# Layer 0 of a graph network: bias rows of two projections added by GpSimd, values projected third, source tile by integer, one-hots from bf16 numbers

## The chip, the core and the metric

The kernel runs on one core of one Trainium2 chip. The core has a matrix engine (TensorE, PE in the profile), VectorE (DVE), ScalarE (ACT), GpSimd (POOL) and a queue for transfers (SyncE, SP). Matrix products land in PSUM, everything else on chip lies in SBUF. The metric is the device time of one execution in microseconds (us). The kernel before takes 1515.7 us, the median of three runs (1515.66 to 1519.37).

## The reference

1250 nodes with 512 features pass through two layers. Each layer adds a graph convolution, a linear attention and a mixture of experts to the features. The change touches the front of layer 0 and the routing in layer 1. Cut to that:

```python
xn = _layernorm(x)                       # x: [1250, 512]
# layer 0, graph convolution: 20000 edges, mean over the edges into a node
h_self = xn @ W_self.T
neigh_sum = segment_sum(xn[src], dst)
h = h_self + (neigh_sum / max(deg, 1)) @ W_neigh.T + bias        # then a layer norm
# layer 0, attention on a normalised row hn
q = sigmoid(hn @ Wq + bq); k = sigmoid(hn @ Wk + bk); v = hn @ Wv + bv
# layer 1 uses the same edges with weights
agg = segment_sum(h1[src] * norm, dst)
# layer 1, experts: the two best of 8 experts for each token, mixed by softmax gates
topk_vals, topk_idx = top_k(logits, 2); gates = softmax(topk_vals)
```

## The kernel before, in words

The nodes are cut into T = 10 tiles of P = 125 rows. The first phase, which the change is about, does two things at once for each tile `t`:

- **Five projections**, listed in `kinds`: y (the neighbour term, applied before the sum over edges), z (the own term), q, k and v. Each is four f32 products of 128 rows by 512 columns into a PSUM tile `pm` (two buffers), and each such product runs as two passes. For z, q, k and v a fifth product `row_vector` adds the bias row: a one-hot column picks one row of `row_parts`, in which every bias row is held as three bf16 parts that `split_rows` makes. ScalarE evicts `pm` into a buffer `o` of a ring with five buffers (a sigmoid for q and k), GpSimd sums q and k into `totals`, and `move_rows` stores `o` to memory in two pieces on SP. y and z work on `xt`, the transposed normalised rows, the others on `ht`, the transposed rows `hr` of a second normalisation; `normal_rows` and `turn` make these for tile t + 1 while tile t is projected.
- **The adjacency matrix** `at`, from the edges: 320 chunks of 125 edges, in 40 groups of 8. For a group VectorE compares the numbers 0 to 127 (`iota_s`) with each edge's row in its source tile (`lo_s`), which gives the one-hot `hs`, and the numbers 0 to 79 with its column (`col_w`), which gives `hm`. ScalarE multiplies `hm` by the top part of the edge weight, GpSimd by two lower parts (line 400). Per chunk PE multiplies `hs` with the parts of `hm` (lines 424 and 427) into one of four PSUM buffers `pa`, and VectorE adds the result into `at` (line 429).

PE's order in this phase is written out by hand: the loop deals out chunks between the projections' products. On the other engines a planner of the framework orders the instructions, by its own costs.

In front of the loop stands the preparation. The edges are loaded, turned into columns (`as_columns`), and VectorE computes each edge's source tile `tile_s` (lines 350 to 352: one comparison per tile boundary, nine in all), the row in it `lo_s`, and the column `col_w`. The five weights and the first rows of x are queued on SP; the weights lie in one large buffer `big`, in the order neighbour, self, q, k, v. Later y and q are loaded back into the same buffer, `reload`, as soon as the weights that lie there are done with.

At the end of the loop the totals are summed over the rows (line 481) and a loop for edges that fit no window follows; it runs no round here, but all engines meet at it, and SP's transfers issued before it have to land. Then come the products with `at` (line 633).

In layer 1 the routing makes lists: for every block of 128 places which token stands where. `listed` makes one-hots of places (`hotp`) and blocks (`blk`), multiplies the blocks by the numbers to be listed (`hotb`), and PE sums them up. The first list gives `row_i`, by which GpSimd gathers rows; the second (`value`: tile, row, a one, and the gate in three bf16 parts, made through `part_b`) gives target rows and gates.

Of the kernel before, what the change touches and what calls it, by code (L numbers as in the profile page):

```python
# [8 lines left out]
F32 = mybir.dt.float32  # L9
# [11 lines left out]
P = 125  # L21
T = N // P
D = 512
# [47 lines left out]
def gps_two_layer_kernel(ctx: ExitStack, tc: tile.TileContext, x, src, dst, ew, rows, cols,  # L71
# [138 lines left out]
    with ExitStack() as phase:  # L210
# [4 lines left out]
        iota_s = gp.tile([CH, 128], F32, name="iota_s")  # L215
# [5 lines left out]
        lo_s = gp.tile([CH, NC], F32, name="lo_s")  # L221
        col_w = gp.tile([CH, NC], F32, name="col_w")
# [6 lines left out]
        full = ring.tile([96, D], F32, name="full", tag="o", bufs=5)  # L229
# [57 lines left out]
        with tc.tile_pool(name="eprep", bufs=1) as ep, \  # L287
# [68 lines left out]
            inside = ep.tile([CH, NC], F32, name="inside", tag="f", bufs=3)  # L356
# [6 lines left out]
            split_rows(row_parts, full, ring, tag="o", bufs=5)  # L363
# [70 lines left out]
        def fill(n):  # L434
            for _ in range(n):
                if fills:
                    m, t = fills.pop()
                    nc.scalar.activation(at[:, m, t, :], zero.to_broadcast([128, NA]), AF.Copy)

        kinds = ((y_d, 0, wn_sb, None, AF.Copy), (z_d, 0, ws_sb, R_GNN, AF.Copy),  # L440
                 (q_d, 1, wq_sb, R_BQ0, AF.Sigmoid), (k_d, 1, wk_sb, R_BK0, AF.Sigmoid),
                 (v_d, 1, wv_sb, R_BV0, AF.Copy))
        steps, step, chunk = T * len(kinds) * DC, 0, 0
        fill(8)
        with tc.manual_schedule(engines={mybir.EngineType.PE}):
            for t in range(T):
                for n, (d, which, w_sb, row, func) in enumerate(kinds):
# [6 lines left out]
                    for c in range(DC):  # L454
                        nc.tensor.matmul(pm, lhs[:, c, :], w_sb[:, c, :], start=(c == 0),  # L455
                                         stop=(row is None and c == DC - 1))
                        if row is not None and c == DC - 1:
                            row_vector(pm, row, False)
                        if c == DC - 1:
                            o = ring.tile([P, D], F32, name="o", bufs=5)  # L460
                            nc.scalar.activation(o, pm, func)
                            move_rows(of_tile(d, t), o)
# [662 lines left out]
    with tc.tile_pool(name="moe", bufs=1) as ep:  # L1125
# [4 lines left out]
        with tc.tile_pool(name="rt", bufs=1) as rt, tc.tile_pool(name="rx", bufs=3) as rx, \  # L1130
                tc.tile_pool(name="rps", bufs=2, space=PSUM) as ps:
            iota_p = rt.tile([P, 128], F32, name="iota_p")
            nc.gpsimd.iota(iota_p, pattern=[[1, 128]], base=0, channel_multiplier=0,
                           allow_small_or_imprecise_dtypes=True)
            edges_b = rt.tile([P, NB], F32, name="edges_b")
# [3 lines left out]
            tok = rt.tile([P, T, 2], F32, name="tok")  # L1139
# [302 lines left out]
```

## Time and profile before

| what | value |
| --- | --- |
| median of the runs | 1515.7 us (1515.66, 1515.70, 1519.37) |
| profiled execution, its own time | 1518.06 us |
| its span, first to last instruction | 1516.4 us |
| mean granted clock of PE | 0.963 |
| DVE `hs`, line 387, 125x1024, median | 1.224 us |
| DVE `hm`, line 394, 125x640, median | 0.817 us |
| DVE addition into `at`, line 429 | 0.319 us, 320 of them |
| POOL low part, line 400, 125x640, median | 1.252 us, 80 of them |
| POOL addition to `totals`, line 468, 125x512, median | 1.404 us, 18 of them |
| ACT eviction, line 461, 125x512, median | 0.597 us |

The page of the profile starts with the busy time of each engine:

```profile
PE 1396.3 (92%) x6082; PEld 873.9 (58%) x6082; DVE 585.7 (39%) x1425; ACT 404.9 (27%) x937; POOL 199.1 (13%) x176
```

and goes on with 40 equal slices of the span. Each digit is the busy share in tenths, so the first eight columns are about the first 300 us:

```profile
PE   5999999999999799999965898898999999999997
DVE  8887777789775683343565000000000000000000
POOL 3355455300000000000005000000000000000000
```

PEld are PE's weight loads, which run beside its products. A row of a group reads: line, engine, operation, output<-inputs, shapes and count, then busy us in all and mean ns of one, then the idle time of that engine just before them and what ended it. A row in order of time begins with the start in us from the span's start and the duration. Durations overlap where an engine starts an instruction before the last one has left it, so what an instruction costs is read from the starts.

### The profile page before, as it was taken

The page shows a single profiled execution, that of the slowest core. Times are in us where ns is not written, and L with a number is a line of the kernel's source. Part 1 is how long each engine was busy: PE and PEld are TensorE (multiplying, and loading weights), DVE is VectorE, ACT ScalarE, POOL GpSimd, SP SyncE. Part 2 cuts the span into 40 slices and gives each one's busy share as a digit, 9 for nine tenths or more (in the row PEclk, how much of TensorE's full clock was granted, in tenths as well). Part 3 has the DMA queues.
Part 4 walks back from the last instruction along what each step waited for, and adds up shares of the span by engine and source line. Part 5 has one row for each costly group of instructions (what it writes and reads, how often), then busy time and mean ns, then how long its engine had stood idle before and what let it go on. Part 6 is the DMA issues. An engine that isn't in the chain of part 4 may idle for free. (4 is left out here: it accounts for less than half of the span.)

```text
span 1516.4 us, 18431 instructions
## 1 busy us (share of the span) xinstructions
PE 1396.3 (92%) x6082; PEld 873.9 (58%) x6082; DVE 585.7 (39%) x1425; ACT 404.9 (27%) x937; POOL 199.1 (13%) x176
## 2 busy tenths in 40 slices
PE   5999999999999799999965898898999999999997
PEld 2445445424554346554534696884767567975673
DVE  8887777789775683343565000000000000000000
ACT  8655455201223422112224121220212012120110
POOL 3355455300000000000005000000000000000000
PEclk9999999999999899999976999999999999999999
DMA  7311111622510130001149456601542106001011
GB/s 223 104 55 56 54 55 49 194 65 89 174 47 11 35 127 1 1 0 41 48 169 340 165 187 235 225 9 38 200 157 82 14 6 233 12 7 14 1 14 15
DMA packets 72765, 134.74 MB, mean 89 GB/s; under 512 B 8328, under 2 KB 9720, under 8 KB 72622
## 3 DMA queue, kind: packets, MB, share of 16 engines
q1 hardware_dynamic: 67694, 122.47, 23.8%
q0 software_dynamic: 4928, 10.43, 3.6%
q8 instruction: 81, 1.33, 0.4%
q14 instruction: 62, 0.51, 0.1%
HBM read 107.27 MB, written 26.38 MB: 88 GB/s over the span
## 5 line engine op out<-in xcount | busy, mean ns | idle before, releaser
L1329 PE MATMUL po<-w,big 128*128 128x512 f32 x576 | 250.1, 592 | 0.0
L1306 PE MATMUL pm<-hts,big 128*128 x960 | 184.8, 355 | 19.7 <-issue 17.3
L1318 DVE TENSOR_SCALAR o<-po,to_gate 128x512 f32<-128x512 f32 (+1 forms) x24 | 17.7, 749 | 454.1 <-PE po L1331 452.8
L1306 PEld LDWEIGHTS pm<-hts,big 128*128 128x128 f32 x960 | 167.0, 196 | 39.5 <-issue 24.1
L1329 PEld LDWEIGHTS po<-w,big 128*128 128x128 f32 x576 | 109.1, 190 | 132.1 <-issue 131.5
L1309 ACT ACTIVATE big<-pm,cols_sb 128x256 f32<-128x256 f32 (+2 forms) x224 | 96.1, 432 | 282.6 <-PE pm L1306 282.4
L1306 PE MATMUL pm<-hts,w 128*128 x832 | 144.8, 336 | 12.6 <-PEq L1389 5.6
L1306 PEld LDWEIGHTS pm<-hts,w 128*128 128x128 f32 x832 | 133.0, 197 | 23.8 <-issue 14.4
L455 PE MATMUL pm<-big,ht 128*125 128x512 f32 x240 | 130.3, 631 | 0.0
L1319 POOL DMA_INDIRECT out_dram<-o,row x24 | 36.9, 1539 | 652.1 <-DVE o L1318 284.9
L429 DVE TENSOR_TENSOR at<-at,pa 128x160 f32 x320 | 102.0, 319 | 41.4 <-PE pa L427 17.6
L400 POOL TENSOR_TENSOR hm<-hm,w_low 125x640 bf16<-125x640 bf16 x80 | 100.3, 1274 | 114.0 <-DVE hm L394 63.4
L123 PE MATMUL pm<-w,at 128*125 128x512 f32 x240 | 114.2, 598 | 0.0
L397 ACT ACTIVATE hm<-hm,w_top 125x80 bf16<-125x80 bf16 x320 | 86.4, 350 | 68.0 <-DVE hm L394 55.1
L633 PE MATMUL pn<-big,at 125*125 125x512 f32 x200 | 92.5, 621 | 3.0 <-DMA big<-q_d 3.0
L455 PE MATMUL pm<-big,xt 128*125 128x512 f32 x160 | 86.8, 633 | 1.2 <-ACT xt L278 1.2
L1309 ACT ACT_TABLE_LOAD x11 | 14.1, 1283 | 255.2 <-PE pm L1306 255.2
L427 PEld LDWEIGHTS <-hs 125*128 125x128 bf16 x640 | 50.8, 97 | 48.8 <-issue 44.0
L424 PE MATMUL pa<-hm,hs 125*128 125x160 bf16 x320 | 64.6, 233 | 12.9 <-DVE at L429 10.9
L424 PEld LDWEIGHTS <-hs 125*128 125x128 bf16 x320 | 31.1, 97 | 67.7 <-issue 38.4
L633 PEld LDWEIGHTS pn<-big,at 125*125 125x125 f32 x200 | 38.5, 196 | 54.7 <-issue 54.6
L427 PE MATMUL pa<-hm,hs 125*128 125x80 bf16 x640 | 64.4, 198 | 0.0
(391 smaller groups left out, 1621.2 us busy)
## 6 DMA issues: line engine op xcount, KB each, us to landing
w<-in_w_dram SPq DMA_DIRECT2D x52, 1024.0 KB
big<-in_w_dram SPq DMA_DIRECT2D x12, 1024.0 KB
x_t<-in_x_dram SPq DMA_DIRECT2D x10, 224.0 KB
xn_d<-xr SPq DMA_DIRECT2D x10, 224.0 KB
y_d<-o SPq DMA_DIRECT2D x10, 224.0 KB
z_d<-o SPq DMA_DIRECT2D x10, 224.0 KB
q_d<-o SPq DMA_DIRECT2D x10, 224.0 KB
k_d<-o SPq DMA_DIRECT2D x10, 224.0 KB
```

The source lines that it names most:

```text
L123: nc.tensor.matmul(ps, lhs[:, c, :], w[:, c, :], start=(c == 0), stop=(row is None and c == DC - 1))
L397: nc.scalar.activation(hm[:, j, 1, :], hm[:, j, 0, :], AF.Copy, scale=w_top[:, g * J + j:g * J + j + 1])
L400: nc.gpsimd.tensor_tensor(hm[:, :, 2 + i, :], hm[:, :, 0, :], w_low[:, i, c8, None].to_broadcast([CH, J, TW]), ALU.mult)
L424: nc.tensor.matmul(pa.rearrange("p k c -> p (k c)"), hs[:, j, :], hm[:, j, 0:2, :].rearrange("p k c -> p (k c)"), start=True, stop=False)
L427: nc.tensor.matmul(pa[:, 1, :], hs[:, j, :], hm[:, j, 2 + i, :], start=False, stop=(i == 1))
L429: add = nc.vector.tensor_tensor(to, to, pa.rearrange("p k (t w) -> p k t w", t=T), ALU.add)
L455: nc.tensor.matmul(pm, lhs[:, c, :], w_sb[:, c, :], start=(c == 0), stop=(row is None and c == DC - 1))
L633: nc.tensor.matmul(pn, at[:P, 0, s, t * P:(t + 1) * P], y[:, s, :], start=(s == 0), stop=(s == T - 1))
L1306: nc.tensor.matmul(pm[:, :width], w1s[e, f // DC][:, c, (f % DC) * 128:(f % DC + 1) * 128], hts[:, c, bass.ds(start, width)], start=(c == ...
L1309: nc.scalar.activation(hid[f][:, :width], pm[:, :width], AF.Gelu, bias=cols_sb[:, C_B11 + e * FC + f:C_B11 + e * FC + f + 1])
L1319: nc.gpsimd.indirect_dma_start(out, bass.IndirectOffsetOnAxis(ap=row[:n], axis=0), o[:n], None, bounds_check=N - 1, oob_is_err=False, comp ...
L1329: nc.tensor.matmul(pm, hid[f][:, s * 128:(s + 1) * 128], w2s[e, f // DC][:, f % DC, :], start=(f == 0), stop=False)
```

## The change

Four things, in one edit:

1. The bias rows of z and v no longer go through PE for each tile. `spread_row` makes each of them once into a full 125x512 tile (one row product and one eviction on ScalarE), and GpSimd adds it to the evicted `o`. For tile 0, z's `o` is held until the rows are spread, after v. The ring of `o` has four buffers instead of five.
2. v is projected third, ahead of q and k, and its weights are queued third.
3. The source tile is computed by one multiplication with conversion to an integer, a conversion back, a comparison and a subtraction, in place of nine comparisons.
4. Numbers that one-hots are made from are held in bf16: `iota_s`, `lo_s`, `col_w`, and in the routing `iota_p`, `edges_a`, `edges_b`, `tok`, `nblk`, `inb`, `blk` and `value`; the gate's parts go straight into `value`.

```diff
-        iota_s = gp.tile([CH, 128], F32, name="iota_s")
+        iota_s = gp.tile([CH, 128], BF16, name="iota_s")
...
-        lo_s = gp.tile([CH, NC], F32, name="lo_s")
-        col_w = gp.tile([CH, NC], F32, name="col_w")
+        lo_s = gp.tile([CH, NC], BF16, name="lo_s")
+        col_w = gp.tile([CH, NC], BF16, name="col_w")
...
-            for i, (o, w) in enumerate(((wn_sb, gw_neigh), (ws_sb, gw_self), (wq_sb, wq0),
-                                        (wk_sb, wk0), (wv_sb, wv0))):
+            for i, (o, w) in enumerate(((wn_sb, gw_neigh), (ws_sb, gw_self), (wv_sb, wv0),
+                                        (wq_sb, wq0), (wk_sb, wk0))):
...
-            nc.vector.tensor_scalar(tile_s, src_c, float(P), None, op0=ALU.is_ge)
-            for t in range(2, T):
-                nc.vector.scalar_tensor_tensor(tile_s, src_c, float(t * P), tile_s,
-                                               op0=ALU.is_ge, op1=ALU.add)
+
+            tile_i = ep.tile([CH, NC], I32, name="tile_i", tag="f", bufs=3)
+            nc.vector.tensor_scalar(tile_i, src_c, 0.5, 1.0 / P, op0=ALU.add, op1=ALU.mult)
+            nc.vector.tensor_copy(tile_s, tile_i)
+            up = ep.tile([CH, NC], F32, name="up", tag="f", bufs=3)
+            nc.vector.scalar_tensor_tensor(up, tile_s, float(P), src_c, op0=ALU.mult, op1=ALU.is_gt)
+            nc.vector.tensor_sub(tile_s, tile_s, up)
...
         kinds = ((y_d, 0, wn_sb, None, AF.Copy), (z_d, 0, ws_sb, R_GNN, AF.Copy),
-                 (q_d, 1, wq_sb, R_BQ0, AF.Sigmoid), (k_d, 1, wk_sb, R_BK0, AF.Sigmoid),
-                 (v_d, 1, wv_sb, R_BV0, AF.Copy))
+                 (v_d, 1, wv_sb, R_BV0, AF.Copy),
+                 (q_d, 1, wq_sb, R_BQ0, AF.Sigmoid), (k_d, 1, wk_sb, R_BK0, AF.Sigmoid))
+        spread = {}
+
+        def spread_row(row):
+            pm = ps.tile([P, D], F32, name="pm")
+            row_vector(pm, row, True, stop=True)
+            spread[row] = hmp.tile([P, D], F32, name=f"spread{row}", bufs=1)
+            nc.scalar.activation(spread[row], pm, AF.Copy)
...
                     for c in range(DC):
+                        in_psum = func is AF.Sigmoid
                         nc.tensor.matmul(pm, lhs[:, c, :], w_sb[:, c, :], start=(c == 0),
-                                         stop=(row is None and c == DC - 1))
-                        if row is not None and c == DC - 1:
+                                         stop=(not in_psum and c == DC - 1))
+                        if in_psum and c == DC - 1:
                             row_vector(pm, row, False)
                         if c == DC - 1:
-                            o = ring.tile([P, D], F32, name="o", bufs=5)
+                            o = ring.tile([P, D], F32, name="o", bufs=4)
                             nc.scalar.activation(o, pm, func)
-                            move_rows(of_tile(d, t), o)
+                            if row is not None and not in_psum:
+                                if t == 0 and n == 2:
+                                    spread_row(R_GNN)
+                                    spread_row(R_BV0)
+                                    nc.gpsimd.tensor_add(held, held, spread[R_GNN])
+                                    move_rows(of_tile(z_d, 0), held)
+                                if t == 0 and n == 1:
+                                    held = o
+                                else:
+                                    nc.gpsimd.tensor_add(o, o, spread[row])
+                            if t > 0 or n != 1:
+                                move_rows(of_tile(d, t), o)
...
-                blk = rt.tile([P, T, 2, nb], F32, name="blk", tag="blk")
+                blk = rt.tile([P, T, 2, nb], BF16, name="blk", tag="blk")
...
-            value = rt.tile([P, T, 2, 6], F32, name="value")
+            value = rt.tile([P, T, 2, 6], BF16, name="value")
...
             for i in range(3):
-                nc.vector.tensor_copy(part_b, left)
-                nc.vector.tensor_copy(value[:, :, :, 3 + i], part_b)
+                nc.vector.tensor_copy(value[:, :, :, 3 + i], left)
```

More of the change, by code (lines that the diff above doesn't have):

```diff
@@ L228, in gps_two_layer_kernel @@
         x_t = {}
-        full = ring.tile([96, D], F32, name="full", tag="o", bufs=5)
+        full = ring.tile([96, D], F32, name="full", tag="o", bufs=4)
         nc.gpsimd.memset(full, 0.0)
@@ L349, in gps_two_layer_kernel @@
             nc.gpsimd.tensor_tensor(w_low[:, 1, :], less, w_low[:, 0, :], ALU.subtract)
-            nc.vector.tensor_scalar(tile_s, src_c, float(P), None, op0=ALU.is_ge)
-            for t in range(2, T):
-                nc.vector.scalar_tensor_tensor(tile_s, src_c, float(t * P), tile_s,
-                                               op0=ALU.is_ge, op1=ALU.add)
+            tile_i = ep.tile([CH, NC], I32, name="tile_i", tag="f", bufs=3)
[4 more added lines that the diff above has]
+            nc.vector.tensor_sub(tile_s, tile_s, up)
             nc.vector.scalar_tensor_tensor(lo_s, tile_s, float(-P), src_c, op0=ALU.mult, op1=ALU.add)
             nc.vector.scalar_tensor_tensor(src_c, tile_s, float(W), where, op0=ALU.mult, op1=ALU.add)
-            inside = ep.tile([CH, NC], F32, name="inside", tag="f", bufs=3)
+            inside = ep.tile([CH, NC], F32, name="inside")
             nc.vector.tensor_scalar(inside, where, float(W), None, op0=ALU.is_lt)
@@ L362, in gps_two_layer_kernel @@
             nc.vector.memset(row_parts, 0.0)
-            split_rows(row_parts, full, ring, tag="o", bufs=5)
+            split_rows(row_parts, full, ring, tag="o", bufs=4)
             for i in range(3):
@@ L1131, in gps_two_layer_kernel @@
                 tc.tile_pool(name="rps", bufs=2, space=PSUM) as ps:
-            iota_p = rt.tile([P, 128], F32, name="iota_p")
+            iota_p = rt.tile([P, 128], BF16, name="iota_p")
             nc.gpsimd.iota(iota_p, pattern=[[1, 128]], base=0, channel_multiplier=0,
                            allow_small_or_imprecise_dtypes=True)
-            edges_b = rt.tile([P, NB], F32, name="edges_b")
+            edges_b = rt.tile([P, NB], BF16, name="edges_b")
             nc.gpsimd.iota(edges_b, pattern=[[1, NB]], base=0, channel_multiplier=0,
                            allow_small_or_imprecise_dtypes=True)
-            tok = rt.tile([P, T, 2], F32, name="tok")
+            tok = rt.tile([P, T, 2], BF16, name="tok")
             nc.gpsimd.iota(tok[:, :, 0], pattern=[[0, T]], base=0, channel_multiplier=1,
@@ L1143, in gps_two_layer_kernel @@
                            allow_small_or_imprecise_dtypes=True)
-            edges_a = rt.tile([P, NA_B], F32, name="edges_a")
+            edges_a = rt.tile([P, NA_B], BF16, name="edges_a")
             nc.gpsimd.iota(edges_a, pattern=[[1, NA_B]], base=0, channel_multiplier=0,
@@ L1183, in listed @@
                 nc.vector.tensor_single_scalar(slot_i, slot_i, 127, op=ALU.bitwise_and)
-                nblk = rt.tile([P, T, 2], F32, name="nblk", tag="nblk")
+                nblk = rt.tile([P, T, 2], BF16, name="nblk", tag="nblk")
                 nc.vector.tensor_copy(nblk, nblk_i)
-                inb = rt.tile([P, T, 2], F32, name="inb", tag="inb")
+                inb = rt.tile([P, T, 2], BF16, name="inb", tag="inb")
                 nc.vector.tensor_copy(inb, slot_i)
-                blk = rt.tile([P, T, 2, nb], F32, name="blk", tag="blk")
+                blk = rt.tile([P, T, 2, nb], BF16, name="blk", tag="blk")
                 nc.vector.tensor_tensor(blk, nblk[:, :, :, None].to_broadcast([P, T, 2, nb]),
@@ L1270, in gps_two_layer_kernel @@
             nc.vector.memset(value[:, :, :, 2], 1.0)
-            part_b = rt.tile([P, T, 2], BF16, name="part_b")
             left = rt.tile([P, T, 2], F32, name="left")
```

## The prediction

> **What bounds the kernel now.** I read the page first: the span is 1516.4 us and TensorE (PE) is busy for 92% of it, so a saved microsecond counts only where PE would otherwise work or wait. Of the change, all but the one-hots of the router lies in layer 0 before its end at about 295 us. The groups of instructions, narrowed to the engine PE and to 28 to 289 us (out<-in, count, then busy us and mean ns, then idle time in front and who ended it), show that stage:
>
> ```profile
> L455 PE MATMUL pm<-big,ht 128*125 128x512 f32 x239 | 129.9, 631 | 0.0
> L424 PE MATMUL pa<-hm,hs 125*128 125x160 bf16 x319 | 64.4, 233 | 12.9 <-DVE at L429 10.9 <-ACT o L461 1.1 <-ACT hm L397 0.5
> L101 PE MATMUL pm<-row_parts,row_pick 96*125 96x512 bf16 x39 | 15.1, 386 | 6.9 <-DVE row_parts L115 6.9
> ```
>
> See the last field. PE waits 12.9 us in front of the edge products, nearly all for VectorE (DVE) to add an earlier product into `at`, and 6.9 us once for the bias rows. The busy times per stretch, from 36 to 290 us, say how full the others are:
>
> ```profile
> 36.00:290.00 254.00, 240.65 (x1443) 126.08 (x1444) 196.16 (x441) 132.76 (x413) 122.15 (x97) 1.00 0.25 75
> ```
>
> After the stretch's length come PE 240.65, weight loads, DVE 196.16, ScalarE (ACT) 132.76, GpSimd (POOL) 122.15 of 254 us. PE sets the end, DVE is near behind, POOL is half idle.
>
> **Part 1, bias rows leave PE.** Of the 40 row products L101 in the loop, those of the own term z and of v go (20), and two come back to spread the rows once. What one costs PE is not its 0.38 us, which overlaps its neighbours, but the distance to the next start. From the order in time of PE (start, duration):
>
> ```profile
> 274.63 0.38 PE L101 MATMUL pm<-row_parts,row_pick 96*125 96x512 bf16 x1
> 274.85 0.23 PE L424 MATMUL pa<-hm,hs 125*128 125x160 bf16 x1
> ```
>
> That is 0.22 us. For tiles 1 to 9, 18 products go: 18 x 0.22 = **-4.0 us**, on the path, since PE bounds there. Tile 0's are in the ramp (part 3).
>
> In their place POOL gets 20 additions of 125x512. The nearest row is POOL's `totals` addition of the same shape, median 1.40 us (1.26 to 2.25): 28 us more on an engine with 132 us free. Two costs can come out. First, delay: POOL works in order, and an addition in front of a group's two low-part products (L400, 2.46 us) makes the group late. Setting each group's L400 end against PE's first use, I find between 0.28 and 3.5 us of slack from group 2 on, mostly 0.6 to 2.7. Today 3 of 18 additions have an L400 queued straight behind them with no gap, and PE never waits for it. In the list of POOL's instructions after the change each addition stands in front of a group that PE first uses 4.9 us or more after the addition's own projection ends; eviction 0.6, addition 1.4 and L400 2.46 make 4.5. So the order is tight in two places and wrong in none: +0.5 us, between 0 and 3.
>
> Second, contention. The order in time shows what POOL does to DVE:
>
> ```profile
> 116.13 0.82 DVE L394 TENSOR_TENSOR hm<-iota_s,col_w 125x640 bf16<-125x640 f32 x1
> 124.03 1.66 DVE L394 TENSOR_TENSOR hm<-iota_s,col_w 125x640 bf16<-125x640 f32 x1
> 123.19 1.82 POOL L468 TENSOR_TENSOR totals<-totals,o 125x512 f32<-125x512 f32 x1 [2.32 <-ACT o L461]
> ```
>
> The same DVE instruction takes 0.84 us more when an addition runs beside it, and the addition 0.4 more. The Trainium skill speaks against this part here: "GPSIMD Engine Reference", section "Specifications", says that POOL's memory interfaces are shared with VectorE and contended when VectorE reads two operands from SBUF. It gives no price; the rows do. In 36 to 290 us the one-hots L387 and L394 lie 38 x (0.059 + 0.088) = 5.6 us above their medians, and xr and hr (0.87 and 0.90 us, against 0.54 alone) 5.9 us: 11.5 us of DVE for 122 us of POOL. For 28 us more that is 2.6 us of DVE. DVE has slack and four buffers `pa`, so I take half for PE: **+1.3 us**. Bounds: 0, and by the rule with every addition hitting a one-hot 20 x 0.84 = 17 us.
>
> The ring `o` falls from 5 to 4 buffers. An `o` is made each 5.1 us and is held for eviction, addition and store, under 10 us; four are 20 us: nothing.
>
> **Part 2, one-hots from bf16 numbers.** The rows are one element a cycle: `hs` (L387, 1024 elements) 1.22 us, `hm` (L394, 640) 0.82 us, so 384 elements in 0.40 us. The change makes all operands 2-byte. The skill has two rules: "VectorE: DVE Perf Modes", "The perf-mode tier table", gives a bf16 tensor_tensor twice the rate; "Vector Engine (DVE) Microarchitecture Reference", section 5.1, says that a two-source instruction with 2-byte operands whose one input is a single element read again and again ran at the single rate. `lo_s` and `col_w` are just that: one number per chunk, repeated along the innermost axis. By the first rule DVE would lose 512/960 + 320/960 = 0.87 us per group, 35 us in all, and most of the 10.9 us of PE waits would go. By the second nothing changes. No row here has this form on DVE, and the second names the very case: **0**, bounds -9 and 0.
>
> **Part 3, the ramp.** The order in time, PE then DVE, at the start:
>
> ```profile
> 28.05 0.59 PE L101 MATMUL pm<-row_parts,row_pick 96*125 96x512 bf16 x1 [6.89 <-DVE row_parts L115]
> 36.41 0.65 PE L132 MATMUL pt<-ident,hr 125*128 125x125 f32 x4 [2.31 <-DVE hr L270]
> 30.04 1.21 DVE L253 TENSOR_TENSOR r<-mv,r 125x2 f32<-125x2 f32 x1
> 35.41 1.41 DVE L270 TENSOR_SCALAR hr<-x_t,mv,r 125x512 f32<-125x512 f32 x2
> ```
>
> PE waits 6.89 us for `row_parts` and 2.31 us for tile 1's `hr`. With v third and without its row, PE goes on at 21.2 with 8 passes of 0.43 us, so 3.4 us of projection move into the first wait. Its weights are there: the third load was issued at 15.36, and SP, whose next store waits for that load, goes on at 20.79. The tile index loses nine DVE instructions (0.31 + 8 x 0.56 = 4.8 us) and gains four (two of 0.31, two of 0.47: 1.6): -3.2. With the first `hs` (1.2 us) now behind `row_parts`, that is ready at about 24 and not 28. But the next wait, for `hr`, is set by DVE. Its new order puts after `row_parts` one set of statistics, two `hs` and two `hm` (4.9 us), then the chain from L253 to `hr`, in before 30.04 to 36.1 = 6.1 us with POOL beside it. 24.3 + 4.9 + 0.4 + 6.1 = 35.7 against 36.1. One projection, k or now q, then remains on either side. **-0.5 us**, bounds -3 (POOL out of the way) and +1.5. The spread evictions (2 x 0.6 us on ACT) lie in this wait; SP's queue meets z's store later, as in before (33.6). In the smaller ring z's eviction waits for `full`, free at 24: hidden too, 0.6 us if not.
>
> **Part 4, the joint.** k comes last instead of v. The chain behind it, ACT 0.6, POOL's total 1.27, PE 1.1, DVE 0.65, ends 4.1 us after the last projection; all engines are released later still, when SP's last loads have landed:
>
> ```profile
> 290.49 0.74 SPq L107 DMA_DIRECT2D v_d<-o  x2
> 294.78 2.07 PE L633 MATMUL pn<-big,at 125*125 125x512 f32 x2 [3.02 <-DMA big<-q_d]
> 294.00:295.00 1.00, 0.22 (x1) 0.56 0.00 0
> 295.00:300.00 5.00, 5.00 (x6) 0.50 0.74 214
> ```
>
> SP has two pieces of q instead of one to issue before that point, 0.4 us apart: **+0.4 us**, bounds 0 and 1.5. The last two rows (0.56 and 0.50 are the granted clock) show a second price: after this 3.0 us gap PE runs at half speed for about 6 us, 3 us lost. "TensorE: Matmul & The Clock Gate", Part 1, asks for a whole idle window of 3.4 us; the trace throttled with less, so the trace decides. Now k's total falls into the middle of the gap, and the clock may stay up: 0 or -3, taken as 0.
>
> **Part 5, the router.** The list chain on DVE ends with `row_i` at 793.14 and the gathers start at 793.59. Two of the removed copies (0.17 us, 0.09 apart where they interleave) stand before it: **-0.3 us**; between -2 (lists at double rate) and 0.
>
> **Sum.** -4.0 + 0.5 + 1.3 + 0 - 0.5 + 0.4 - 0.3 = -2.6 us. The profiled execution took 1518.06 us, 1.7 more than its span and 2.4 above the median 1515.7 (runs 1515.66 to 1519.37, about a clock loss of 3 us apart). So 1515.5 for it, and against the median **1513.1 us**. About 0.3%, 4.5 us, is what a measurement of this kernel can tell from no change.
>
> **Rivals.**
> (A) The forecast, 1513.1, its own range 1510 to 1516; 0.45.
> (B) All the saving lands. POOL hides (-1.8) and the joint keeps its clock (-3): 1508.3. For it speaks that PE never waits for L400 today; against it that the clock also fell after a window with 1 us of work. 0.25.
> (C) The bf16 one-hots do run double: waits for `at` fall by 8, the router by 1.7: 1503.4. 0.06.
> (D) Slower, by one mechanism: POOL holds DVE at the one-hots, L429 comes late, and PE, out of `pa` buffers, stops. Each hit costs 0.84 us. The forecast becomes a loss when 4 of the 20 additions do so beyond the share counted; 12 give 1513.1 + 10.1 = 1523.2. For it: DVE is 77% busy and most PE waits are DVE's already; against: today's 18 additions leave 10.9 us of such waits altogether. 0.24.
>
> Faster by over 0.3% (below 1511.2) are most of B, C and a little of A: 0.32. Slower (above 1520.2) is half of D: 0.14. The rest, 0.54, is within. The range 1506.5 to 1520 leaves out C and D's tail.
>
> **What would show it.** L101 falls to 22 in this stage, with PE busy about 4 us less. L387 and L394 stay at 1.22 and 0.82 us (else C). The wait for `at` stays near 11 to 13 us; 20 would be D. PE waits for L400 nowhere. Tile 1's `hr` transposes start near 36. The clock after the joint tells A from B.

## The result and the profile after

The kernel after takes **1532.69 us**, the median of five runs (1530.71 to 1533.67), against 1516.0 us for five runs of the kernel before in the same comparison. The ratio is **1.0106, with a 95% interval of 1.0093 to 1.0119**: slower by about 16 us. A second comparison of the same two kernels, under "The experts' part", gave 1.0143. The forecast was 1513.1 us and no change.

The page after begins with the engines and, cut to three rows of slices, with where they are busy:

```profile
PE 1397.2 (91%) x6064; PEld 873.0 (57%) x6064; DVE 596.7 (39%) x1417; ACT 411.4 (27%) x943; POOL 229.9 (15%) x196
...
PE   5899899899999799999964899898999998999997
DVE  8787787698776673344475000000000000000000
POOL 4355666500000000000005000000000000000000
```

PE has 18 products fewer and the same busy time; DVE has 11 us more and POOL 31 us more. To see where the span grew, the order in time of PE gives the start of the same products in both kernels:

| stage, bounded by PE's products | before | after | difference |
| --- | --- | --- | --- |
| start to the first edge product | 41.4 us | 46.4 | +5.0 |
| edge loop: first to last edge product | 248.3 | 254.5 | +6.3 |
| joint: to the first product with `at` (633, now 657) | 5.1 | 5.8 | +0.7 |
| products with `at` | 113.9 | 110.7 | -3.2 |
| attention, up to the router's first rank product | 375.3 | 375.5 | +0.2 |
| router and experts, to the end of the span | 732.4 | 738.0 | +5.6 |
| span | 1516.4 | 1531.0 | +14.6 |

Three stages carry the loss, and the last of them runs code that the change leaves as it is but for the number formats of the router's lists. The groups of PE from 36 to 305 us answer to the first lines shown of before:

```profile
L427 PE MATMUL pa<-hm,hs 125*128 125x160 bf16 x320 | 65.7, 234 | 20.4 <-DVE at L432 19.5
...
L101 PE MATMUL pm<-row_parts,row_pick 96*125 96x512 bf16 x20 | 7.6, 381 | 0.0
```

The row products did go, and PE waits nowhere for a low part. But in front of the edge products PE now waits 19.5 us for DVE's addition into `at`, where it was 10.9. The groups of DVE, with shapes kept apart, over the same stretch show DVE's own side:

```profile
L432 DVE TENSOR_TENSOR at<-at,pa 128x160 f32 x320 | 102.0, 319 | 44.2 <-PE pa L430 20.6 <-DVE at L432 7.0 <-PE pm L101 0.9
L390 DVE TENSOR_TENSOR hs<-iota_s,lo_s 125x1024 bf16<-125x1024 bf16 x38 | 51.3, 1351 | 11.6 <-PE pa L430 11.4
L397 DVE TENSOR_TENSOR hm<-iota_s,col_w 125x640 bf16<-125x640 bf16 x38 | 39.6, 1043 | 0.0
```

The same rows before, over 36 to 290 us:

```profile
L387 DVE TENSOR_TENSOR hs<-iota_s,lo_s 125x1024 bf16<-125x1024 f32 x38 | 48.7, 1283 | 14.3 <-PE pa L427 14.2
L394 DVE TENSOR_TENSOR hm<-iota_s,col_w 125x640 bf16<-125x640 f32 x38 | 34.4, 905 | 0.0
```

The means were 1283 ns for `hs` and 905 for `hm`, and are 1351 and 1043. The medians have not moved (1.23 and 0.82 us): a few instructions have become long. Of 38 `hm`, four took 1.66 us before; now ten take 1.66 to 1.70. Of 38 `hs`, four took more than 1.5 us before; now eight. The order in time shows one of the new ones with its cause and its consequence:

```profile
124.40 1.27 POOL L484 TENSOR_TENSOR o<-o,spread 125x512 f32<-125x512 f32 x1 [0.99 <-ACT o L474]
124.65 1.70 DVE L397 TENSOR_TENSOR hm<-iota_s,col_w 125x640 bf16<-125x640 bf16 x1
124.88 0.23 PE L427 MATMUL pa<-hm,hs 125*128 125x160 bf16 x1 [1.04 <-DVE at L432]
128.41 0.23 PE L427 MATMUL pa<-hm,hs 125*128 125x160 bf16 x1 [1.35 <-DVE at L432]
```

POOL adds the bias, the one-hot beside it takes 0.88 us longer than its median, the additions into `at` queued behind it on DVE come late, and PE has no free buffer `pa`.

### The profile page after: what moved, and what is told of

It reads as the page before. It is cut to its first block, busy times and chain, and to the rows that moved or that the text cites. A ratio compares the mean times of both kernels' runs of the same rounds, so it can differ in the third digit from the quotient of the medians.

```text
span 1531.0 us, 18440 instructions
## 1 busy us (share of the span) xinstructions
PE 1397.2 (91%) x6064; PEld 873.0 (57%) x6064; DVE 596.7 (39%) x1417; ACT 411.4 (27%) x943; POOL 229.9 (15%) x196
## 5 line engine op out<-in xcount | busy, mean ns | idle before, releaser
L657 PE MATMUL pn<-big,at 125*125 125x512 f32 x200 | 89.4, 604 | 1.8 <-DVEq L516 1.8
L427 PE MATMUL pa<-hm,hs 125*128 125x160 bf16 x320 | 65.7, 234 | 20.4 <-DVE at L432 19.5
L1331 ACT ACT_TABLE_LOAD x11 | 14.1, 1283 | 257.8 <-PE pm L1328 257.8
L427 PEld LDWEIGHTS <-hs 125*128 125x128 bf16 x320 | 31.0, 97 | 80.5 <-issue 45.9
```

Source lines behind the costliest of these rows:

```text
L427: nc.tensor.matmul(pa.rearrange("p k c -> p (k c)"), hs[:, j, :], hm[:, j, 0:2, :].rearrange("p k c -> p (k c)"), start=True, stop=False)
L657: nc.tensor.matmul(pn, at[:P, 0, s, t * P:(t + 1) * P], y[:, s, :], start=(s == 0), stop=(s == T - 1))
L1331: nc.scalar.activation(hid[f][:, :width], pm[:, :width], AF.Gelu, bias=cols_sb[:, C_B11 + e * FC + f:C_B11 + e * FC + f + 1])
```

## The experiments

Theories at the outset: **T1**, the additions on POOL hold DVE, and PE pays in its waits for `at`; **T2**, one-hots from bf16 numbers run slower beside POOL; **T3**, the new order with v third spoils the start. **T4** and **T5** came later, about the last stage. Every kernel was timed beside the kernel before on the same chip; its median there was 1516.5, 1513.2, 1516.0, 1514.8 and 1515.6 us in the five sittings.

### Which part of the change it is

Four kernels. The change with the bias rows put back on PE and no addition on POOL:

```diff
-                        in_psum = func is AF.Sigmoid
+                        in_psum = row is not None
```

> The kernel after with the bias rows of z and v back on PE and no additions on GpSimd; v third, the integer tile index, bf16 and the ring of four stay. Theory 1 (GpSimd's additions hold VectorE, and PE waits for the additions into `at`): PE's wait there goes back from 19.5 to 10 to 12 us, tile 1's first edge product back from 46.4 to about 41, time 1514 to 1518 us. Theory 2 (the bf16 one-hots are slower beside GpSimd): the wait stays near 19 us, time 1528 to 1533. Theory 3 (the new order with v third spoils the start): the loop is as before but the first edge product stays at 45 to 46, time about 1521.

The other way round, the kernel before with bf16 numbers and with POOL's additions from tile 1 on (v stays last, the nine comparisons stay):

```diff
+                    in_psum = row is not None and (t == 0 or func is AF.Sigmoid)
...
+                            if row is not None and not in_psum:
+                                nc.gpsimd.tensor_add(o, o, spread[row])
```

> The kernel before with bf16 one-hots and, from tile 1 on, the 18 additions of z and v on GpSimd (rows spread at the end of tile 0, ring of four); v last, nine comparisons. Theory 1: the start as before (first edge product at about 41.4), the loop longer by 18/20 of 10.3 us less the 4.0 saved, so 5 us: about 1521 us, PE's wait for `at` near 19 us. Theory 2: the same loop loss, but bf16 alone shows it too. Theory 3: time as before, 1512 to 1516.

The kernel before with the bf16 numbers alone (the declarations of the change, nothing else):

> The kernel before with only the numbers of the one-hots in bf16, in layer 0 and in the routing. Theory 1: `hs` and `hm` stay at 1.22 and 0.82 us at the median, time 1515 to 1517, PE's wait for `at` 10 to 12 us. Theory 2: longer means of `hs` and `hm` and a wait for `at` above 15 us, time 1520 to 1526.

The kernel before with v projected and loaded third alone (two lists reordered):

> The kernel before with only v projected third and its weights queued third; bias rows stay on PE. Theory 1 and 2: time 1514 to 1518; the first edge product within 1 us of 41.4; the joint after the loop 0.4 to 1 us longer, or 2 to 3 us shorter where the clock stays up. Theory 3: first edge product at 44 to 46 us, time 1519 to 1521.

| kernel | median us | ratio to before (95%) | start | edge loop | PE waits for `at` |
| --- | --- | --- | --- | --- | --- |
| rows back on PE | 1520.85 | 1.0033 (1.0021 to 1.0044) | 43.9 | 249.2 | 13.5 |
| additions and bf16 | 1532.61 | 1.0110 (1.0093 to 1.0127) | 42.0 | 255.9 | 19.4 |
| bf16 alone | 1516.2 | 1.0005 (0.9996 to 1.0014) | 41.5 | 248.2 | 10.9 |
| v third alone | 1516.89 | 1.0017 (1.0004 to 1.0029) | 42.1 | 248.9 | 13.3 |

bf16 numbers change nothing: `hs` 1283 ns and `hm` 905 ns in the mean, as before. T2 falls. T3 is worth 0.4 us by the medians and 0.6 to 4.4 by the interval; its start is 0.7 us later. The additions alone bring 16.4 us over bf16 alone, with nearly the same waits (19.4 us) as in the kernel after. The two profiles lie 14.8 us apart: 7.7 us in the loop, 1.8 at the joint and 7.3 in the router and the experts, less 2.6 in the products with `at`; the rest is small. Some 4.6 us over bf16 alone remain when the additions are taken out of the change; 2.4 of them are the start, below. T1 had put these two kernels lower, at about 1521 and at 1514 to 1518 us. The two losses do not simply add up: the kernel after has the late start, but a loop, a joint and a last stage that are 1.1 to 1.7 us shorter than with the additions alone.

### Row products and additions, each with and without the other

Without both (the output lacks the bias in those 18 results):

```diff
-                                nc.gpsimd.tensor_add(o, o, spread[row])
```

> The additions kernel without the 18 GpSimd additions, so with neither row products nor additions from tile 1 on: the output lacks the two bias rows in those 18 results. Measured so far: with row products and no additions 1516.2 us (edge loop 248.2, experts' part 667.2); with additions and no row products 1532.6 (edge loop 255.9, experts' part 675.1). If the additions alone cost the time (T1), the loop falls to 248.2 - 4.0 = 244.2 and the experts' part stays at 667: about 1512.5. If the experts' part grows because 18 instructions (with their weight loads) are gone from TensorE's stream (T4), it is 674 here too, and the time about 1519 to 1520.

With both (those results get their bias twice):

> The additions kernel with the 18 row products kept as well, so that these 18 results have their bias twice. TensorE's stream is as long as before. T1 (additions alone cost): loop 255.9 + 4.0 = about 260, experts' part 675 as with the additions: about 1536. T4 (the experts' part follows TensorE's instruction count): loop 260, experts' part 667: about 1528.

| edge loop, us | no additions | 18 additions on POOL |
| --- | --- | --- |
| row products on PE | 248.2 | 256.4 |
| no row products | 246.8 | 255.9 |

Read across, the additions cost 8.2 to 9.1 us. The 8.2 hold 1.1 us for the two products that spread the rows: these run inside the loop in all of the four but the first, bf16 alone, which has none. Read down, taking the row products away gains 1.4 us without additions and 0.5 us with them, not 4.0. The starts of PE's products show where the rest went. The steps from a row product to the next start fall from 8.1 to 5.3 us without additions (the 5.3 hold the two spreads), and from 9.3 to 5.3 with them. The steps from an edge product to the next start grow by 1.4 us without additions and by 2.9 with them. So where DVE is late anyway, a row product fills a wait, and a part of what PE saves comes back between the edge products. The time of the kernel with neither is 1515.55 us, ratio 1.0010 (0.9995 to 1.0025), so no gain was seen even with nothing in the products' place. (Without the biases the experts get other tokens, so this total bounds less than its loop does.)

Then what it is about an addition that costs. The same instruction with one input instead of two (bias left out), and the addition on DVE, straight from PSUM in place of ScalarE's copy:

```diff
-                                nc.gpsimd.tensor_add(o, o, spread[row])
+                                nc.gpsimd.tensor_scalar(o, o, 1.0, None, op0=ALU.mult)
```

> The 18 GpSimd additions turned into a multiplication of the same tile by 1.0, with one input in place of two (output lacks the bias of these 18 results). If any GpSimd instruction on such a tile holds VectorE's two-operand instructions (T1), the time stays within 2 us of 1532.6 and the 1024-element one-hots stay near 1.37 us. If it is the second input that does it, they fall to 1.28 and the time to that of the kernel with neither row products nor additions. If part of the cost is only that results leave later through one more engine, that part stays.

```diff
-                            nc.scalar.activation(o, pm, func)
+                            if row is not None and not in_psum:
+                                nc.vector.tensor_add(o, pm, spread[row])
+                            else:
+                                nc.scalar.activation(o, pm, func)
```

> The 18 results leave the products' buffer through VectorE with the bias added on the way, in place of ScalarE's copy and GpSimd's addition. VectorE gets 18 x about 0.7 us = 13 us, GpSimd and ScalarE lose theirs. T1: no hold by GpSimd, so the one-hots are back at 1.28 and 0.90 us, the additions' 13 us reach TensorE in half at most: loop 244 to 251, and the time 1512 to 1519 if the experts' part stays at 667, 7 us more if it follows TensorE's count (T4).

One input: 1525.54 us (1.0078, 1.0052 to 1.0104), loop 251.5. T1 had put the time within 2 us of 1532.6. So a second input is not what it takes, though with it the hold is about double. On DVE: 1524.91 us (1.0078, 1.0048 to 1.0108), loop **257.8**, against the 244 to 251 I expected. DVE's groups show why this was no way out:

```profile
L387 DVE TENSOR_TENSOR hs<-iota_s,lo_s 125x1024 bf16<-125x1024 bf16 x38 | 49.3, 1297 | 10.7 <-PE pa L427 10.3
L394 DVE TENSOR_TENSOR hm<-iota_s,col_w 125x640 bf16<-125x640 bf16 x38 | 34.4, 904 | 0.0
L471 DVE TENSOR_TENSOR o<-pm,spread 125x512 f32<-125x512 f32 x18 | 12.4, 688 | 6.4 <-PE pm L464 4.8 <-PE pa L427 1.1 <-DMA big<-q_d 0.3
```

The added holds are gone (904 ns, as without additions), but the additions' own 12.4 us cost the loop 11.0. That DVE is 77% busy and idle now and then did not give it slack.

### How the hold goes with POOL's work

Three sizes and the opposite direction: each addition on half of the columns (half of the bias left out); in two halves, nothing left out; the kernel before with bf16 numbers without the 18 additions into `totals` (so that the sums hold the first tile only); and the same kernel, complete, with POOL's work in shorter pieces.

```diff
-                                nc.gpsimd.tensor_add(o, o, spread[row])
+                                nc.gpsimd.tensor_add(o[:, :D // 2], o[:, :D // 2], spread[row][:, :D // 2])
```

> The additions kernel with each of the 18 GpSimd additions on 256 of the 512 columns (output lacks half of the bias there). Measured so far, VectorE's extra time in the two one-hots, xr and hr and its own additions over the kernel with neither row products nor additions, and the edge loop over that kernel's 246.8 us: one-input GpSimd instruction +5 us and +4.7; two-input addition +9.8 and +9.1; addition on VectorE +12.6 and +11.0. T1 (each us that VectorE loses reaches TensorE nearly whole): half the columns hold about half as long, +4 to +6 us in VectorE and as much in the loop: 251 to 253. If the hold goes by the count of GpSimd instructions and not by their length, loop 255 to 256.

```diff
+                                for half in (slice(0, D // 2), slice(D // 2, D)):
+                                    nc.gpsimd.tensor_add(o[:, half], o[:, half], spread[row][:, half])
```

> The additions kernel (1532.6 us, loop 255.9) with each of the 18 bias additions in two instructions of 256 columns, the whole bias added. T1 with the hold by one instruction's length: VectorE's extra 2 x 2.6 = 5.2 us in place of 9.8, loop 250.5 to 252. If the hold goes by the sum: VectorE's extra 9.8 us or more, loop 256 to 258.

```diff
-                                else:
-                                    nc.gpsimd.tensor_add(s, s, o)
```

> The kernel before with bf16 numbers (1516.2 us, loop 248.2) with the 18 GpSimd additions into totals left out (the sums of q and k then hold the first tile alone). The same mechanism in the other direction, without a single addition of the change in it: T1: the one-hots fall from 1.28 and 0.905 us towards 1.22 and 0.80, VectorE gains 6 to 10 us and the loop falls by as much: 239 to 243, time 1506 to 1511. If instead the additions of the change cost by the order in which they make VectorE work, or by what follows them in the later stages, nothing or up to 2 us comes here.

```diff
+                                    for half in (slice(0, D // 2), slice(D // 2, D)):
+                                        nc.gpsimd.tensor_add(s[:, half], s[:, half], o[:, half])
...
+                for j in (0, J // 2):
+                    part = slice(g * J + j, g * J + j + J // 2)
+                    nc.gpsimd.tensor_tensor(hm[:, j:j + J // 2, 2 + i, :], hm[:, j:j + J // 2, 0, :],
+                                            w_low[:, i, part, None].to_broadcast([CH, J // 2, TW]), ALU.mult)
```

> The kernel before with bf16 numbers, with GpSimd's work cut into shorter instructions: each of the 18 additions into totals in two of 256 columns, each of the 80 low parts in two of four chunks. No bias addition in it. 18 additions of 256 columns held VectorE for 2.6 us in all (loop +2.0 us) and of 512 columns 9.8 us (loop +9.1), so the hold grows faster than the length; leaving out the 18 additions into totals took 5.5 us off the loop. If the hold goes by the length of one instruction (T1): the one-hots fall from 1.28 and 0.905 us towards 1.22 and 0.82, the loop from 248.2 by 2 to 6 us, time 1510 to 1515, under both kernels. If it goes by the sum of GpSimd's time: the sum grows by some 8 + 15 us of fixed cost, loop 250 to 254.

For every kernel the next table sums DVE's busy time in `hs`, `hm`, `xr`, `hr` and, where it has them, in bias additions, and sets what it has over a reference against what the loop has over the same one. The reference (98.1 us, loop 246.8) has neither row products nor additions; for the last three it is bf16 alone (98.2 us, loop 248.2). Of the +8.2 us with row products, 1.1 are the two spreads.

| kernel | DVE's time over the reference | edge loop over the reference |
| --- | --- | --- |
| addition on 256 columns | +2.6 | +2.0 |
| one input, 512 columns | +5.2 | +4.7 |
| two pieces of 256 columns | +7.0 | +6.2 |
| 512 columns | +9.8 | +9.1 |
| addition on DVE | +12.6 | +11.0 |
| row products and 512 columns | +7.9 | +8.2 |
| no additions to `totals` | -7.5 | -5.4 |
| `totals` and low parts in pieces | -3.6 | -1.5 |

Each microsecond that DVE loses reaches PE at 0.8 to 1.0, and one that it gains gives back less, 0.4 to 0.7. T1 stands, in both directions and with no addition of the change in the last two rows. Another order of work is not the reason: between the first and the last edge product DVE's 430 instructions, and ACT's, stand in one and the same order in the reference and in the first four kernels of the table, and likewise in bf16 alone and without the additions to `totals`. Without the additions to `totals` DVE's groups read:

```profile
L429 DVE TENSOR_TENSOR at<-at,pa 128x160 f32 x320 | 102.2, 319 | 41.9 <-PE pa L427 19.3 <-DVE at L429 6.2 <-PE pm L101 1.2
L387 DVE TENSOR_TENSOR hs<-iota_s,lo_s 125x1024 bf16<-125x1024 bf16 x38 | 46.6, 1225 | 16.0 <-PE pa L427 15.9
L394 DVE TENSOR_TENSOR hm<-iota_s,col_w 125x640 bf16<-125x640 bf16 x38 | 31.1, 818 | 0.0
```

Mean and median now agree: not one of the 76 one-hots is long, although POOL still makes its 80 low parts (100 us). In the loop the low parts hold no one-hot (in the start one does take 1.87 us beside them, below), and the additions into `at` take 319 ns in this kernel as in all others. All of the long one-hots of the kernel before came from the 27 us of `totals`. (This kernel's total, 1545.3 us, can't be compared: with other sums the router picks other experts, and its last stage takes 767 us.)

My sizes for these kernels missed twice. Half the columns gave loop 248.8 (1524.39 us, 1.0052, 1.0035 to 1.0069), less than the 251 to 253 expected; two halves gave 253.0, more than the 250.5 to 252 that twice the half would be. Shorter pieces help a little, but their sum counts as well. So the kernel with everything in pieces, meant to beat both, ended at 1515.04 us, ratio 0.9999 (0.9988 to 1.0009): its loop is 1.5 us shorter and its time is that of the kernel before. With the additions in halves, 1530.25 us, 1.0112 (1.0087 to 1.0137).

### The start

The kernel before with bf16 numbers and the integer tile, with four buffers `o` and with five:

```diff
-            nc.vector.tensor_scalar(tile_s, src_c, float(P), None, op0=ALU.is_ge)
...
+            nc.vector.tensor_scalar(tile_i, src_c, 0.5, 1.0 / P, op0=ALU.add, op1=ALU.mult)
```

> The kernel before with bf16 numbers, the source tile by integer, and four result buffers in place of five; v last and the row products as before. The kernel that has all of the change but the additions took 1520.85 us, 4.6 more than bf16 alone, with the first edge product at 43.9 us in place of 41.5; third place for v alone gave 42.1 and 1516.9. If the integer tile (fewer instructions on VectorE, so another order of its work at the start) or the four buffers bring the rest: first edge product at 43 to 44, time 1518 to 1520. If it is the combination with v third: 41.5 and 1516.

> The kernel before with bf16 numbers and the source tile by integer, with the five result buffers of before. With four buffers the first edge product came at 45.9 us and the time was 1520.9; without the integer tile and with five buffers 41.5 and 1516.2. Integer tile as the cause: 45 to 46 again and 1519.5 to 1521. Ring of four as the cause: 41.5 and 1516.

1520.91 us (1.0034, 1.0024 to 1.0044) with four and 1520.20 (1.0038, 1.0026 to 1.0049) with five; first edge product at 45.9 and 45.7 us, loop 248.0 and 248.3. It is the integer tile, by itself, and not the ring. It does what it should: `row_parts` is ready 2.3 us earlier (PE's row product starts at 25.80 and not 28.12). What follows is seen in the order in time of the kernel with five buffers, POOL first:

```profile
28.62 6.49 POOL L403 TENSOR_TENSOR hm<-hm,w_low 125x640 bf16<-125x640 bf16 x4 [6.16 <-DMA x_t<-in_x_dram]
29.52 1.87 DVE L397 TENSOR_TENSOR hm<-iota_s,col_w 125x640 bf16<-125x640 bf16 x1
...
31.51 1.02 DVE L253 TENSOR_TENSOR r<-mv,r 125x2 f32<-125x2 f32 x1
32.45 1.55 DVE L267 TENSOR_SCALAR xr<-x_t,mv,r 125x512 f32<-125x512 f32 x1
33.92 1.20 DVE L254 TENSOR_TENSOR r<-r,r 125x2 f32<-125x2 f32 x1
```

Both groups' one-hots now stand ahead of tile 1's statistics, so POOL runs its four low parts in one piece, 28.6 to 35.1, right beside the chain to `hr`. Before, they fell into two pairs with a gap:

```profile
29.15 3.30 POOL L400 TENSOR_TENSOR hm<-hm,w_low 125x640 bf16<-125x640 bf16 x2 [8.91 <-DMA x_t<-in_x_dram]
33.61 2.46 POOL L400 TENSOR_TENSOR hm<-hm,w_low 125x640 bf16<-125x640 bf16 x2 [1.17 <-DVE r L249]
```

Two-column instructions (0.15 us when alone) take more than 1 us. PE waits 2.59 us for `xr` and 3.96 for `hr`, its clock falls (mean 0.60 in 35 to 40 us, 0.77 in 40 to 46; bf16 alone has 1.00 in both), and the next eight passes take 5.21 us and not 3.60. In the kernel after the two bias additions of tile 0 come on top, 33.7 to 36.3, and the first edge product is at 46.4 (45.1 when the same kernel was profiled again). Adding v third to the integer tile (rows back on PE) gave 43.9, better than the integer tile alone; why was not tried.

### The experts' part

It is the same code, yet 5.6 us longer. First, whether it is the kernel's own: after once more, unchanged.

> The kernel after once more, unchanged. From the first product of the router's ranks to the end it took 738.0 us, before 732.4. If the trace's waits there are the program's own, they come again at the same places within 1 us (6.0 at the fourth expert's code, 1.5 us in the second) and the part takes 737 to 739; if they differ from run to run, the part varies by several us, and the difference of the two profiled runs says nothing. Time 1532 to 1534, first edge product 46.4, loop 254.5.

1536.3 us (1.0143, 1.0120 to 1.0167), this part 738.6 us: it comes again. The loss as a whole is larger here, 21 us and not 16, and the two intervals don't meet. Between the two profiles of this one kernel the start went from 46.4 to 45.1 us, the products with `at` from 110.7 to 113.8 and the attention from 375.5 to 378.3, while the loop stayed at 254.5; so in those three stages a difference of 1 to 3 us between two kernels says little. The -3.2 us of the products with `at` is PE's clock after the joint, which goes either way in the same kernel (mean 0.84 here over 290 to 312 us and 0.92 there).

T4: the waits at the head of an expert's code, for which the trace shows no releaser ("issue"), go by where the code lies in PE's program; the change takes 18 products and their weight loads, 36 instructions, out in front of it. T5: they come with the additions. Here are PE's first products of the seventh of the eight experts (the expectations call it the fourth) in before, after, and the kernel with row products and additions both, in the order in time:

```profile
1263.04 22.74 PE L1306 MATMUL pm<-hts,w 128*128 x128 [2.71 <-issue]
```

```profile
1277.81 22.37 PE L1328 MATMUL pm<-hts,w 128*128 x121 [5.95 <-issue]
```

```profile
1268.08 22.72 PE L1318 MATMUL pm<-hts,w 128*128 x128 [2.64 <-issue]
```

In the eight kernels that keep the row products in place this wait is 2.64 to 2.71 us, with additions or without. It is 5.95 to 6.07 us in the five that have GpSimd's additions in their place and PE's products in the same order here (after twice, 512 columns, two halves, half the columns), and 4.55 in the one with the addition on DVE. T5 falls for this wait, since the kernel with both has the additions and 2.64 us. Then the place was moved by itself, with transposes that nobody reads at PE's very beginning: 36 in the kernel after, 92 and 220 in the kernel before.

```diff
+            pe = eps.tile([CH, NC // R, R], F32, name="pe")
+            for _ in range(36):
+                nc.tensor.transpose(pe[:32, 0, :32], ident[:32, :32], ident[:32, :32])
             normal_rows(0)
```

> The kernel after with 36 transposes of 32x32 before everything else on TensorE, whose results nobody reads, while TensorE waits for the first tile anyway. From the first product of the router's ranks to the end the kernels with row products or with the addition on VectorE took 731 to 732 us, the kernel after 738.0 and the additions kernel 739.7, in code that is the same, with more waits for which the trace shows no cause where an expert's code begins (6.0 in place of 2.7 us at one of them). TensorE's program is 36 instructions shorter there. T4 (where the experts' code lies in the program sets these waits): with the 36 put back this part falls to 731 to 733 and the time to 1525 to 1528. T5 (it comes with the additions): it stays at 738, time 1532.

> The kernel before with 92 transposes of 32x32 ahead of everything else on TensorE, whose results nobody reads (36 of them took 2.1 us, so 92 take 5.4, inside the 8.15 us for which TensorE waits for the first tile). Nothing of the change is in it. T4 (the place of the experts' code in TensorE's program sets the waits at an expert's start; the profile shows instruction packets of 8 KB and of 16 KB): if the place counts in steps of 128 instructions, 92 more is the same as 36 fewer, and the wait of 2.7 us at the fourth expert becomes 6.0, the part from the ranks' first product to the end 735 to 740 in place of 732.4. If the place doesn't matter: 2.7 and 732 to 733, time 1515 to 1518.

> The same with 220 transposes (12.8 us, about 5 us more than the wait that hides them). If the place counts in steps of 256 instructions, 220 more is the same as 36 fewer: 6.0 us at the fourth expert, the part 735 to 740. If in steps of 128, the same in both. If the place doesn't matter: 2.7, 732 to 733. The start pays some 4 to 6 us here in every case.

Each transpose is a product and a weight load, as the profile of the first of these kernels shows, so it counts as two instructions where the expectations count one:

```profile
1.61 1.94 PEld L312 LDWEIGHTS pe<-ident 32*32 32x32 f32 x36 [1.61 <-POOL ident masks.py:199]
1.61 2.10 PE L312 MATMUL pe<-ident 32*32 32x32 f32 x36 [1.61 <-POOL ident masks.py:199]
...
1280.43 19.81 PE L1331 MATMUL pm<-hts,w 128*128 x110 [2.65 <-issue]
```

The 36 transposes are 72 instructions, twice what the change takes out, and with them the wait in after is 2.65 us again. With 184 or 440 instructions (92 or 220 transposes) more in before, and nothing of the change, it becomes 5.65 and 5.59:

```profile
1273.21 22.97 PE L1309 MATMUL pm<-hts,w 128*128 x128 [5.65 <-issue]
```

So T4 is shown for this wait: instructions far in front of it, whose results nothing uses, change it by about 3 us. By what rule the place counts stays open. The steps of 128 instructions that the expectations speak of were not tested, because of the double count. Nor is the place all: the addition on DVE has as many products and weight loads as the additions on POOL with bf16, and 4.55 us where they have 6.02.

For the whole part T4 is not enough. With the 36 transposes it took 736.9 us, not 731 to 733, since the fourth expert's wait grew from 6.2 to 10.0 us, and the time stayed at 1534.3 us (1.0109). In before it became 733.5 with 92 transposes and 736.6 with 220. Those totals (1528.4 and 1521.1 us) can't be used, as the planner arranged the start anew: first edge product at 51.0 and 40.1. The waits over 0.5 us from the first expert's products to the end sum up to 32.0 us before and 34.7 after: 3.2 more at the seventh expert, 1.5 in the sixth where there was none, 1.5 less at the fourth, the rest small. In the second profile of after the 3.2 come again, the 1.5 in the sixth do not. PE's mean granted clock over this part was 0.94 after and 0.95 before. Only the 3.2 us are explained; the rest of the 5.6 stays open.

## Why the prediction was wrong, step by step

- **"18 x 0.22 us = -4.0 us, on the path, since PE bounds there."** The 18 products went and the price of one was read correctly: from the kernel with rows back on PE to the kernel after, the steps behind the row products in the loop fall from 8.1 to 4.2 us. But the path was not PE's alone. Measured: -1.4 us in the loop without additions (-2.5 without the two spreads that run in it there), -0.5 with them, where 2.9 of the 4.0 us came back between the edge products.
- **"Contention ... 2.6 us of DVE ... I take half for PE: +1.3 us."** This is the step that failed, in both factors. DVE's four kinds of instruction lost 9.5 us in the kernel after. With the additions alone they lost 9.8, and the loop took 9.1 of these, not half. The first factor: I divided 11.5 us of seen excess by all 122 us of POOL. 100 of those are low parts, which hold no one-hot in the loop; leaving out the 27 us of `totals` took 7.5 us off DVE. So the price is 7.5 / 27 = 0.28 us per us of addition, not 0.09, and the 27 us of new ones paid 0.36. The second factor: I read DVE's 77% as slack. An engine that alternates with PE through four buffers has little slack at the place where it is held.
- **Rival D had the mechanism.** "20 would be D": the wait became 19.5. It counted 12 hits more; with the additions alone seven more `hm` and five more `hs` are long. It lacked the start and the experts' part, and I gave it 0.24, because today's 18 additions "leave 10.9 us of such waits altogether". They do, and without them 6.4 are left: those 18 alone already cost 5.4 us of loop. (Half of D's 0.24, the chance that I gave for more than 1520.2 us, is 0.12 and not 0.14.)
- **The rule.** "GPSIMD Engine Reference", "Specifications", pointed at this cost, and I let an average from the trace overrule it. For 18 additions the rule with every one hitting a one-hot gives 18 x 0.84 = 15.1 us of DVE and my price 2.3; 9.8 was found, nearer to the rule.
- **"+0.5 us" for late low parts:** PE waits for none in the kernel after. Right at 0, within its bounds.
- **One-hots from bf16: 0.** Right: 1.0005 with 0.9996 to 1.0014, `hs` 1283 ns. "Vector Engine (DVE) Microarchitecture Reference", section 5.1, held, and the tier table did not. The router's -0.3 us can't be seen either (router and experts take 732.4 us in that kernel and before).
- **The ramp: "-0.5 us, bounds -3 and +1.5".** It was +5.0, and +3.7 in the second profile. The early `row_parts` came, though later than forecast (25.7 us, about 24). The step that failed is "the chain from L253 to `hr`, in before 30.04 to 36.1 = 6.1 us with POOL beside it": I carried over its length, while POOL's low parts, set free earlier, closed up to one block beside it. It began at 31.5 and not 29.6, since `row_parts` and a held `hm` came late, and from its beginning to tile 1's `hr` transposes passed 7.6 us where it was 6.4 before. They began at 39.1 and not near 36. And PE's clock fell in the waits (0.50 over 35 to 40 us): the eight passes behind took 5.48 us and not 3.60, which the sum did not have at all.
- **The joint: "+0.4 us".** It was +0.7, within its bounds, and with the clock after it "0 or -3": both were met, in two profiles of the same kernel.
- **Nothing in the sum stood for code that the change doesn't touch.** It brought 5.6 us, of which the experiments explain 3.2.

## What to carry to other kernels

Before moving work to GpSimd, find out which of its present instructions cause VectorE's long ones and divide by their time alone; then look for what VectorE will be doing when the new ones come. Where two engines alternate over a few buffers, count what the second one loses nearly whole: here it was 0.8 to 1.0 of it, at 77% busy. And try the removal by itself first: here the kernel without row products and without additions has a loop only 1.4 us shorter, and no gain in its time. The kernel before was not beaten by any version tried.

## What the runs showed of the hardware

- GpSimd held VectorE also where one of the two had one input: 18 GpSimd instructions with one input took 1.718 us each and cost VectorE 5.2 us (two inputs: 1.500 us each, 9.8). A two-column `tensor_scalar` on VectorE (line 249) took 1.19 us in the start of the kernel after beside GpSimd and 0.15 before. The 128x160 addition from PSUM was never held: 318 or 319 ns in every kernel.
- A GpSimd addition of 256 columns took 0.958 us in the mean and one of 512 columns 1.500: two halves take 0.42 us more than the whole.
- TensorE's waits at the head of dynamically reached code changed by about 3 us with instructions added or removed about a thousand microseconds earlier: from 2.71 to 5.65 and 5.59 with 184 and 440 more, and from 5.95 to 2.65 with 72 more.
